# A query buffer of its own for the first cross unit of a layer, and its maxima dealt earlier

## The chip, the cores and the metric

The kernel runs on one core of one Trainium2 chip. The metric is the device time of one execution in microseconds (us), of which the median of three runs counts. The engines are named as the profile names them: PE is the matrix engine (PEld its weight loads), DVE the vector engine, ACT the scalar engine, POOL GpSimd, and SP the engine that only issues DMAs.

## The reference

Two layers of a transformer block run over four batches of 512 tokens with 320 features. Each layer has self attention, cross attention to a context of 1601 rows with 192 features, and a gated feed-forward part; each part has a layer norm before it and a residual add behind it. There are 20 heads of 16 features.

```python
h1 = _ln(x, n1_g, n1_b)
x = _attn(h1, h1, q1, k1, v1, o1_w, o1_b, heads) + x
h2 = _ln(x, n2_g, n2_b)
x = _attn(h2, context, q2, k2, v2, o2_w, o2_b, heads) + x
h3 = _ln(x, n3_g, n3_b)
a, g = jnp.split(h3 @ ff_w1 + ff_b1, 2, axis=-1)
ff = a * jax.nn.gelu(g, approximate=False) @ ff_w2 + ff_b2
return ff + x
```

`_attn` is softmax attention: `a = softmax(q k^T / 4)`, `out = a v`, and then `out @ wo + bo`. Queries times keys are kept nearly exact: a value is split into a high and a low part, and both are multiplied in the fast format fp32r.

## The kernel before

**Units.** The work of a layer is cut into 20 self units, 20 cross units and 4 feed-forward units. An attention unit is one batch and one group of four heads (five groups to a batch). A self unit has 4 chunks of 128 keys, a cross unit 13 (1601 keys). Below, self unit 0 to 19 and cross unit 0 to 19 are counted within a layer.

**What a unit needs.** Before a unit runs, three things are made for it: its queries (`queries`, L726 to L740) and keys (`keys`, L758, or `keys_of_context`, L801), each as matmuls, a copy to a staging tile, a split into high and low part on POOL (L627, L628) and DMAs on SP's queue into a query buffer and a key buffer; and the maximum of each query's scores, which softmax subtracts. For the maxima the scores are multiplied once with queries as rows (matmuls into tile `sps`, L957) and reduced by DVE (L978; L1000 for the last keys). `max_end` (L1029 to L1037) sends the maxima through a transpose and eight small DMAs into a row tile `m`.

**A unit's own run (`main`).** In each chunk the scores are multiplied again with keys as rows (tile `st`, L1144, two matmuls for each head), a third matmul subtracts the maxima (L1147), ACT takes the exponential into a place of a ring of buffers (L1157), and a chunk later the products with the values follow (tile `av`, L1171). The first chunk's product is copied into the unit's output tile `o` (L1182, on ACT); those of later chunks are copied to a place (L1187) and added by POOL (L1188). When the last chunk is added, `add_finish` transposes `o` on DVE, divides by the row sums, and four DMAs carry it from `o` to tile `aT` (L1072), from which the output projection reads (L1081). The tile `o` comes from a pool of three buffers.

**Maxima beside scores.** A chunk has two half rounds: scores of heads 0 and 1, then of heads 2 and 3. `giver` deals one group of maxima matmuls (four matmuls, two heads, one block of 512 keys) to each half round. They use the other half of the array's rows, so they run beside the scores. A self unit has 8 half rounds, and the next self unit has 8 groups of maxima, so the slots are just full. A cross unit has 26 groups. What does not fit is dealt as an extra round: two groups, eight matmuls, with no scores beside them, and three reductions on DVE (one of two heads, two of one head). The banks that they fill come from the pools `ps_m` (two double banks) and `ps_st` (four banks, which the scores and most other work also use).

**The first cross unit.** Cross unit 0 of each layer (`u.early`) needs 26 groups while only self units run before it. Its keys are due at the start of the unit four before it, with 16 rounds between the two pieces; its two query pieces are due at the start of the unit two before it (L847), since its query buffer is one of four that units take in turn, and is free only when the unit four before it in the order of attention has its scores (`unread`). In `giver`, maxima of this unit are dealt only when queries and keys have been made and moved for three rounds (`at_hand`).

**The planner.** Everything beside a unit's own run stands in queues (`add(chain, cost, f, due, ...)`). After each chunk `steps` takes pieces of work by due time as long as its credit lasts; `pace` sets the credit from the total of what is due. Each engine's order is thus fixed when the program is built.

Of the kernel before, what the change touches and what calls it, by code (L numbers as in the profile page):

```python
# [64 lines left out]
def kernel(ctx: ExitStack, tc: tile.TileContext, x, context, ws, out):  # L65
# [57 lines left out]
    def load_x(b):  # L123
# [33 lines left out]

    own = const.tile([P, 7, N], F32, name="pr")
    mine = [own[:, i, :] for i in range(7)]
    places = {  # L160
        "self": mine + [w1_flat[:, (2 * KB + 2) * D : (2 * KB + 2) * D + N], w1r[:, 4 * CTX : 4 * CTX + N]],
        "cross": mine + [wself[:, i * N : (i + 1) * N] for i in range(5)],
    }
    at_place = {"kind": "self", "i": -1}

    def place():
# [130 lines left out]
    for i, u in enumerate(attn):  # L297
# [10 lines left out]
        else:  # L308
            part = u.m % 4 if u.m < B * G - 1 else 0
            u.kT, u.k0 = (kbuf[0], part * N) if part < 3 else (kbuf[2], 0)  # L310
            u.other = attn[i - 3] if u.m == B * G - 1 else attn[i - 4] if u.m > 3 or u.m == 3 and u.l else None
        u.qbuf = qbuf[i % 4]
        u.mrow = mrows[i % 2]
# [359 lines left out]
    def add_proj(u):  # L673
# [5 lines left out]
        keys_due, apart = (  # L679
            (units[u.i - 4].start, 8) if u.early else (lead(u) - 5, 3) if u.m == 1 else (due - 10, 4)  # L680
        ) if u.cross else (due, 0)
# [153 lines left out]
        def unread():  # L835

            return u.n < 4 or attn[u.n - 4].scored == attn[u.n - 4].nch

# [4 lines left out]
        def add_queries():  # L843
            if u.g == 0 and u.cross:
                add(chain, 0.0, hold, due - 4, yes, lambda: "h" in u.own)
            for part in range(parts):
                add(chain, (0.05 + 0.427 / parts,) * 3, lambda part=part: queries(part), units[u.i - 2].start if u.early else due - 2, unread)  # L847

# [280 lines left out]
    def main(u, give, nxt):  # L1129
# [34 lines left out]
        def values(c):  # L1164
# [15 lines left out]
            if c == 0:  # L1180
                u.o = three.tile([P, N], F32, tag="o", name="o")
                (nc.vector.tensor_copy if last else nc.scalar.copy)(u.o, ps)  # L1182
            elif last:
                nc.vector.tensor_tensor(u.o, ps, u.o, ALU.add)
            else:
                vo = place()
                nc.scalar.copy(vo, ps)  # L1187
                nc.gpsimd.tensor_tensor(u.o, u.o, vo, ALU.add)  # L1188
# [58 lines left out]
    def ff_main(u, give, nxt):  # L1247
# [16 lines left out]
        hc = one.tile([P, 5, N], F32, tag="ctxT", name="hid")  # L1264
        hid = [hc[:, i, :] for i in range(5)]

        def full(c, pss, ahead):
# [24 lines left out]
        def gate(c, pss):  # L1292
            gl = mine[5 + c % 2]
            nc.scalar.activation(gl, pss[1], AF.Gelu, bias=b1[:, NHC + c : NHC + c + 1])  # L1294
# [231 lines left out]
```

## Time and profile before

| what | value |
|---|---|
| time, median of 3 runs | 3206.76 us (3204.16 to 6031.88) |
| span of the profiled execution | 3212.3 us |
| PE busy | 3036.1 us, 95% |
| DVE busy | 2093.8 us, 65% |
| ACT busy | 1963.7 us, 61% |
| POOL busy | 1267.8 us, 39% |

The profile gives the profiled execution's span, from its first to its last instruction, as its own time; nothing else of that execution is told. A unit's borders can be found in the trace by its score matmuls (L1144): a self unit has 32 of them, a cross unit 104. So a table of windows with such borders tells what each engine did while one unit ran. A row of it has the window and its length, then for PE, PEld, DVE, ACT and POOL the busy time and the number of instructions, then the clock that PE was granted (1.00 is full speed), the share of the DMA engines and the GB/s that they moved. Where the window table is asked for one line of the kernel alone, the busy times are those of that line.

### The profile page before, as it was taken

Reading aid. Unit: us, or ns where it says so; the run is one execution under the profiler, and the core shown is the slowest. Engines: PE = TensorE matmul, PEld = TensorE weight load, DVE = VectorE, ACT = ScalarE, POOL = GpSimd, SP = SyncE. Lnnn points to the kernel's source line nnn. Section 1 sums busy time; section 2 is a strip of 40 time slices with the busy share of each in tenths; the row PEclk is TensorE's granted clock in tenths of the full one; section 3 lists DMA queues with packets and bytes.
Section 4 is the critical chain, followed back from the end, with each engine's and each line's share of the span. In section 5 each row is a group of like instructions: output and inputs, shape, how many; then the busy total and the mean of one; then the engine's idle time right before and its main releaser. Section 6 shows DMA issues by size and latency. Waiting matters only on the chain.

```text
span 3212.3 us, 92658 instructions
## 1 busy us (share of the span) xinstructions
PE 3036.1 (95%) x37842; PEld 1644.5 (51%) x37842; DVE 2093.8 (65%) x2869; ACT 1963.7 (61%) x4029; POOL 1267.8 (39%) x1449
## 2 busy tenths in 40 slices
PE   8899899999999999999998998999999999999999
PEld 4455555555454555455454554555555555544555
DVE  6777778778678767522256777787777777784221
ACT  3666557777777778711136665587777778785110
POOL 3445334544544544211124453345454454442000
PEclk8999989999999999999999999999999999999999
DMA  4433212211211211200113322121111211212000
GB/s 96 94 71 77 54 37 49 59 37 40 56 38 38 57 35 27 85 1 5 27 30 78 73 60 52 39 53 40 32 46 40 40 44 34 40 23 66 9 11 15
DMA packets 256579, 145.32 MB, mean 45 GB/s; under 512 B 150037, under 2 KB 246681, under 8 KB 256153
## 3 DMA queue, kind: packets, MB, share of 16 engines
q1 hardware_dynamic: 254888, 138.33, 19.5%
q8 instruction: 298, 4.88, 0.7%
q10 hardware_dynamic: 1264, 1.06, 0.2%
q14 instruction: 129, 1.05, 0.1%
HBM read 33.04 MB, written 7.93 MB: 13 GB/s over the span
## 4 chain that ended last, share of the span: by engine, by line
PE 77%; DVE 6%; ACT 6%; SPq 4%; DMA 3%; issue 2%; POOL 1%; ACTq 0%; POOLq 0%; DVEq 0%
PE av L1171 19%; PE st L1144 16%; PE fps L1271 9%; PE st L1147 6%; PE yps L1327 5%; PE sps L957 4%; ACT pr L1157 3%; PE ops L1081 3%; PE qps L726 3%; PE kps L801 3%; PE vps L900 3%; DVE pm L978 2%; SPq L1037 2%; PE fps L1284 2%; DVE nmax L978 2%
## 5 line engine op out<-in xcount | busy, mean ns | idle before, releaser
L978 DVE TENSOR_REDUCE pm<-sps 128x2 f32<-128x1024 f32 (+1 forms) x980 | 1132.3, 1195 | 166.5 <-PE sps L957 155.6
L1157 ACT ACTIVATE pr<-st 128x512 f32<-128x512 f32 (+1 forms) x1710 | 906.7, 602 | 259.7 <-PE st L1147 250.6
L1144 PE MATMUL st<-q,kT 32*128 32x512 f32 (+1 forms) x5440 | 1001.0, 443 | 44.5 <-ACT w L810 26.8
L957 PE MATMUL sps<-kT,q 32*128 32x512 f32 (+1 forms) x6400 | 989.2, 410 | 31.2 <-DVE pm L978 11.3
L1188 POOL TENSOR_TENSOR o<-o,pr 128x512 f32<-128x512 f32 x359 | 461.2, 1285 | 750.4 <-ACT pr L1187 728.1
L1144 PEld LDWEIGHTS st<-q,kT 32*128 32x128 f32 (+1 forms) x5440 | 504.6, 184 | 471.3 <-ACT pr L1157 149.7
L1171 PE MATMUL av<-pr,vals 128*32 128x512 f32 (+1 forms) x3420 | 657.2, 629 | 40.5 <-ACT pr L1157 21.0
L1147 PE MATMUL st<-m,units 2*128 2x512 f32 (+1 forms) x2720 | 614.2, 402 | 24.4 <-DMA m<-turned 23.3
L1157 ACT ACTIVATE wself<-st 128x512 f32<-128x512 f32 (+1 forms) x867 | 462.9, 603 | 103.2 <-PE st L1147 101.6
L957 PEld LDWEIGHTS sps<-kT,q 32*128 32x128 f32 x6400 | 483.4, 190 | 68.7 <-DVE pm L978 27.8
L978 DVE TENSOR_REDUCE nmax<-sps 128x2 f32<-128x1024 f32 (+1 forms) x340 | 378.4, 1153 | 157.2 <-PE sps L957 117.2
L1171 PE MATMUL av<-wself,vals 128*32 128x512 f32 (+1 forms) x1734 | 376.3, 621 | 14.2 <-ACT pr L1157 14.0
L1188 POOL TENSOR_TENSOR o<-o,wself 128x512 f32<-128x512 f32 x191 | 245.2, 1284 | 342.1 <-ACT wself L1187 339.9
L1147 PEld LDWEIGHTS st<-m,units 2*128 2x128 f32 (+1 forms) x2720 | 313.4, 185 | 70.8 <-issue 30.9
L1271 PE MATMUL fps<-hT,w 128*128 128x512 f32 x640 | 285.3, 598 | 1.4 <-DVE hid L1297 0.9
L1294 ACT ACTIVATE pr<-fps,b 128x512 f32<-128x512 f32 x80 | 50.7, 684 | 385.4 <-PE fps L1284 274.6
L1187 ACT COPY pr<-av 128x512 f32<-128x512 f32 x359 | 217.1, 605 | 25.8 <-PE av L1171 24.2
L1171 PEld LDWEIGHTS av<-pr,vals 128*32 128x32 f32 (+1 forms) x3420 | 92.2, 109 | 215.3 <-ACT pr L1157 92.8
L1271 PEld LDWEIGHTS fps<-hT,w 128*128 128x128 f32 x640 | 118.5, 190 | 151.6 <-issue 145.6
L627 POOL TENSOR_SCALAR stage<-stage 128x256 fp32r<-128x256 f32 (+1 forms) x155 | 106.8, 689 | 193.9 <-ACT stage L734 97.9
L801 PEld LDWEIGHTS kps<-ctxT,w 32*128 32x128 f32 (+1 forms) x4992 | 115.4, 164 | 53.8 <-ACT pr L1157 28.7
L430 POOL TENSOR_SCALAR root<-root 128x4 f32<-128x4 f32 x23 | 5.2, 226 | 328.0 <-DVE root L424 327.7
(100 smaller groups left out, 3269.0 us busy)
## 6 DMA issues: line engine op xcount, KB each, us to landing
kT<-w SPq DMA_DIRECT2D x240, 104.0 KB
q<-stage SPq DMA_DIRECT2D x320, 64.0 KB
q<-stage SPq DMA_DIRECT2D x154, 128.0 KB
aT<-o SPq DMA_DIRECT2D x320, 32.0 KB
m<-turned SPq DMA_DIRECT2D x636, 2.0 KB
kT<-stage SPq DMA_DIRECT2D x156, 64.0 KB
kT<-w SPq DMA_DIRECT2D x80, 72.0 KB
w<-in_L_xattn_ff_w_dram SPq DMA_DIRECT2D x20, 256.0 KB
```

The source lines that it names most:

```text
L627: eng.tensor_scalar(high.bitcast(F32R), x, 1.0, None, ALU.mult)
L801: nc.tensor.matmul(ps[to : to + n, :PIECE], lhsT=wk_q[rows, k, u.g * GD : u.g * GD + n], rhs=first.kvT[rows, k, at : at + PIECE], start=(k ...
L957: nc.tensor.matmul(out, lhsT=u.q[rows, e, queries].bitcast(F32R), rhs=u.kT[rows, keys].bitcast(F32R), start=(e == 0), stop=(e == 1),)
L978: nc.vector.tensor_reduce(to[:, j : j + n], part, AX.X, ALU.max, negate=(ns == 1))
L1144: nc.tensor.matmul(st[:r, :], lhsT=keys, rhs=u.q[rows, e, :].bitcast(F32R), start=(e == 0), stop=False)
L1147: nc.tensor.matmul(st[:r, :], lhsT=units_of[two_rows, :r].bitcast(F32R), rhs=u.mrow[two_rows, :].bitcast(F32R), start=False, stop=True,)
L1157: nc.scalar.activation(p[:r], st[:r], AF.Exp)
L1171: nc.tensor.matmul(ps[j * SLOT : (j + 1) * SLOT, :], lhsT=columns_of[:r, head : head + SLOT], rhs=pr.pop((c, j))[:r, :], start=True, stop= ...
L1187: nc.scalar.copy(vo, ps)
L1188: nc.gpsimd.tensor_tensor(u.o, u.o, vo, ALU.add)
L1271: nc.tensor.matmul(ps, lhsT=w1[:, k, i * FF + c * P : i * FF + (c + 1) * P], rhs=u.hT[:, k, :], start=ahead and k == 0, stop=not ahead and ...
L1327: nc.tensor.matmul(ps[:, :D], lhsT=hid[c][:, t * P : (t + 1) * P], rhs=w2[:, c, :], start=(c == 0), stop=(c == NHC - 1),)
```

## The change

The kernel after has one more query buffer, `early_q`, for cross unit 0 of each layer. With it the wait on the unit four before goes (`unread`), its two query pieces are due at the start of the unit six before it and four rounds later, and its two pieces of keys at the start of the unit five before it and eight rounds ahead of that. The buffers are paid for with two others: the ring of places loses one of seven (`pr`), for which self units get a place in `w2`'s tile and cross units get none; and the output tiles `o` come from a pool of two buffers instead of three. The feed-forward part's second gate buffer, which was the seventh place, is now taken from the same pool of two.

```diff
-    own = const.tile([P, 7, N], F32, name="pr")
-    mine = [own[:, i, :] for i in range(7)]
+    own = const.tile([P, 6, N], F32, name="pr")
+    mine = [own[:, i, :] for i in range(6)]
     places = {
-        "self": mine + [w1_flat[:, (2 * KB + 2) * D : (2 * KB + 2) * D + N], w1r[:, 4 * CTX : 4 * CTX + N]],
+        "self": mine + [
+            w1_flat[:, (2 * KB + 2) * D : (2 * KB + 2) * D + N],
+            w1r[:, 4 * CTX : 4 * CTX + N],
+            w2_flat[:, 3 * D + 4 * kw : 3 * D + 4 * kw + N],
+        ],
         "cross": mine + [wself[:, i * N : (i + 1) * N] for i in range(5)],
     }
+    early_q = const.tile([P, 2, N], F32, name="early_q")
...
-        u.qbuf = qbuf[i % 4]
+        u.qbuf = early_q if u.early else qbuf[i % 4]
...
-            (units[u.i - 4].start, 8) if u.early else (lead(u) - 5, 3) if u.m == 1 else (due - 10, 4)
+            (units[u.i - 5].start, 4) if u.early else (lead(u) - 5, 3) if u.m == 1 else (due - 10, 4)
...
-            return u.n < 4 or attn[u.n - 4].scored == attn[u.n - 4].nch
+            return u.n < 4 or u.early or attn[u.n - 4].scored == attn[u.n - 4].nch
...
-                add(chain, (0.05 + 0.427 / parts,) * 3, lambda part=part: queries(part), units[u.i - 2].start if u.early else due - 2, unread)
+                add(chain, (0.05 + 0.427 / parts,) * 3, lambda part=part: queries(part), units[u.i - 6].start + 4 * part if u.early else due - 2, unread)
...
-                u.o = three.tile([P, N], F32, tag="o", name="o")
+                u.o = two.tile([P, N], F32, tag="o", name="o")
...
+        gls = [mine[5], two.tile([P, N], F32, tag="o", name="gl")]
...
-            gl = mine[5 + c % 2]
+            gl = gls[c % 2]
```

## The prediction

> **What bounds the kernel now.** I read the head of the page first, then the table of windows, with borders at the first score matmul of a unit, to find where the time of this change lies.
>
> ```profile
> span 3212.3 us, 92658 instructions
> PE 3036.1 (95%) x37842; PEld 1644.5 (51%) x37842; DVE 2093.8 (65%) x2869; ACT 1963.7 (61%) x4029; POOL 1267.8 (39%) x1449
> L1157 ACT ACTIVATE pr<-st 128x512 f32<-128x512 f32 (+1 forms) x1710 | 906.7, 602 | 259.7 <-PE st L1147 250.6
> L1188 POOL TENSOR_TENSOR o<-o,pr 128x512 f32<-128x512 f32 x359 | 461.2, 1285 | 750.4 <-ACT pr L1187 728.1
> L1294 ACT ACTIVATE pr<-fps,b 128x512 f32<-128x512 f32 x80 | 50.7, 684 | 385.4 <-PE fps L1284 274.6
> ```
>
> PE is busy 95% of the span, so over the whole kernel nothing but PE's gaps, and its time at a lowered clock, can be won. The next fence has layer 0's self units 4, 8, 12, and 14 to 19, then cross unit 0, and of layer 1 self unit 0 and self units 18 and 19. Columns: window, length, busy time and count of PE, PEld, DVE, ACT, POOL; then the granted clock, the DMA share and GB/s.
>
> ```profile
> 117.50:138.20 20.70, 18.46 (x205) 8.72 (x200) 17.40 (x25) 11.59 (x24) 6.98 (x7) 0.84 0.30 69
> 197.00:211.10 14.10, 13.23 (x188) 6.84 (x184) 12.26 (x21) 10.20 (x22) 6.36 (x7) 1.00 0.39 87
> 265.80:286.60 20.80, 19.97 (x396) 12.62 (x392) 15.45 (x29) 14.02 (x30) 13.34 (x18) 1.00 0.30 80
> 303.50:318.90 15.40, 14.71 (x212) 7.70 (x208) 12.80 (x18) 11.42 (x25) 7.72 (x8) 1.00 0.43 87
> 318.90:334.00 15.10, 13.18 (x164) 6.16 (x160) 11.25 (x16) 11.05 (x23) 6.96 (x7) 1.00 0.31 63
> 334.00:353.90 19.90, 17.89 (x308) 10.74 (x304) 13.59 (x20) 12.07 (x25) 6.44 (x6) 1.00 0.27 57
> 353.90:368.70 14.80, 13.80 (x228) 8.31 (x224) 10.03 (x15) 10.92 (x23) 6.30 (x9) 1.00 0.19 39
> 368.70:401.10 32.40, 26.70 (x476) 15.54 (x476) 27.34 (x37) 12.27 (x27) 11.66 (x12) 0.84 0.26 52
> 401.10:431.20 30.10, 27.34 (x372) 16.15 (x366) 20.52 (x33) 12.84 (x29) 4.26 (x4) 0.83 0.08 16
> 431.20:483.30 52.10, 48.22 (x750) 28.23 (x742) 38.28 (x47) 34.94 (x73) 24.80 (x23) 0.93 0.24 48
> 1647.10:1671.70 24.60, 22.07 (x233) 10.44 (x232) 20.86 (x27) 11.21 (x22) 4.47 (x6) 0.86 0.22 41
> 1977.30:2009.60 32.30, 27.17 (x474) 15.12 (x474) 27.29 (x37) 12.23 (x27) 11.04 (x11) 0.84 0.27 53
> 2009.60:2039.70 30.10, 27.45 (x373) 17.05 (x366) 20.54 (x33) 12.84 (x29) 4.87 (x6) 0.83 0.08 16
> ```
>
> Units 18 and 19 take 62.5 us in layer 0 and 62.4 in layer 1, where a plain self unit (unit 8) takes 14.1. DVE is busy 27.3 of unit 18's 32.4 us, and the clock is granted at 0.84 and 0.83. The same table for the maxima matmuls alone says why (units 17, 18, 19, columns PE and PEld):
>
> ```profile
> 353.90:368.70 14.80, 4.09 (x24) 1.98 (x24) 1.00 0.19 39
> 368.70:401.10 32.40, 11.22 (x80) 5.18 (x82) 0.84 0.26 52
> 401.10:431.20 30.10, 8.55 (x80) 4.47 (x80) 0.83 0.08 16
> ```
>
> A self unit has slots beside its scores for 32 maxima matmuls; units 18 and 19 have 80 each, so 48 each, six extra rounds of eight, stand alone. These are cross unit 0's. PE's waits in these two units (total, times, longest) and DVE's reductions there name the limit:
>
> ```profile
> PEld sps L957 <- DVE pm L978: 4.2, 5, 1.4
> PEld st L1144 <- DVE pm L978: 4.1, 5, 1.6
> L978 DVE TENSOR_REDUCE pm<-sps x36: 677/932/1227, 371.8 to 428.6; 128x2 f32<-128x1024 f32 x18, 128x1 f32<-128x512 f32 x18
> 377.12 0.86 PE L957 MATMUL sps<-kT,q 32*128 32x512 f32 x8 [0.63 <-DVE nmax L978]
> 316.20:318.90 2.70, 2.45 (x32) 1.15 (x28) 2.58 (x3) 1.94 (x5) 1.29 (x1) 1.00 0.12 22
> ```
>
> Scores (`st`) and maxima (`sps`) wait until DVE has emptied a bank. One extra round is 0.86 us of PE (fourth line, eight matmuls), but one reduction of two heads and two of one head on DVE, by the ends of the third line's range 1.23 + 2 x 0.68 = 2.6 us. The last line is a chunk with nothing beside its scores and eight maxima: 2.7 us, DVE busy 2.58.
>
> **The change part by part.** What the changed kernel's order of instructions shows (an order, no times): in self units 14 to 19 the maxima go from 32, 32, 32, 24, 80, 80 to 40, 40, 48, 48, 48, 48, in cross unit 0 from 136 to 144, in both layers alike. So 12 extra rounds in units 18 and 19 become 10 spread over units 14 to 19 (1, 1, 2, 2, 2, 2), unit 17's eight missing ones fill slots, and cross unit 0 gets a fifth round. Nothing is removed in sum; the question is the price of a round where it now stands.
>
> *Price where it stood.* The order gives each unit's other matmuls (all but scores, maxima, values). Unit 8 has 36 in 14.1 us, unit 12 has 144 in 20.8, both with 32 maxima: 6.7 / 108 = 0.062 us for one. Unit 18 has 156: without extra rounds 14.1 + 120 x 0.062 = 21.5, so its six cost 10.9, 1.8 each. Unit 19 has 102: 18.2, so 11.9 for six, 2.0 each. Together 22.8 us a layer. Unit 4 is unit 8 with two rounds more (36 others): 6.6, 3.3 each, at clock 0.84. Layer 1's unit 0 has 48 others and four rounds: (24.6 - 14.8) / 4 = 2.4, at 0.86.
>
> *Price where it goes.* Four of the ten stand in chunks with 24 to 48 other matmuls (one in unit 15, two in 16, one in 18). Such a chunk has 2.7 + 24 x 0.062 + 0.86 = 5.0 us of PE at least, and DVE has 2.58 + 2.6 = 5.2: DVE just fits, and I take PE's 0.86. Unit 19's two stand with 24 value matmuls, but 3.5 rounds in one chunk, so as before: 2.0. Four stand in chunks with 0 to 12 others (14, 17 twice, 18); there DVE sets the pace, and I take 2.6, DVE's own price, between 0.86 and unit 4's 3.3. Sum 4 x 0.86 + 2 x 2.0 + 4 x 2.6 = 17.8, so **-5.0 us a layer**; ends for all ten: 8.6 and 33. What is late next in units 18 and 19 is PE with 156 and 102 others, less what moved ahead.
>
> *Cross unit 0's fifth round*: 0.86 to 3.3; unit 18's price is nearest, **+1.8**. *Unit 17's slots*: nothing for PE, beside scores; DVE gets two reductions, 2.5 us, in a unit with 10.03 of 14.8 busy. If that cover failed it would be those 2.5.
>
> *Moved queries and keys.* The second piece of keys goes from unit 13 to 12, the queries from 17 to 13, the value matmuls of 16 to 18 a little: 0.062 each, which one unit loses and another gains, so zero. Their 16 DMAs are as many as before. In unit 14, SP's queue then holds eight query DMAs where six others stood, ahead of the eight that carry the maxima of unit 15; at some 0.65 us each (2.88 for four below) these come 1.3 us later. They hide behind the extra round of unit 14's chunk 2 (2.6); without it, 1.3.
>
> *Ring of places.* Cross units have 11 instead of 12, self units nine as before. The exponentials' idle time is ended by scores for 250.6 of 259.7 us (page rows above), none by POOL's add, the slow reader of a place. So nothing; if it did bind, one add, 1.3 us, per chunk.
>
> *Gate buffer of the feed-forward part.* Gelu waits for matmuls, 274.6 of 385.4 us (page row), and still alternates between two buffers: nothing.
>
> *Two output tiles instead of three.* This adds a wait: a unit's first copy into `o` (L1182, ACT) must wait for the four DMAs that empty the tile of the unit two before. They are issued in the same unit's first chunk. Behind the copy on ACT stand the exponentials, and PE's scores wait for their banks. Rows of SP and ACT in layer 0's unit 14 and layer 1's unit 4:
>
> ```profile
> 308.20 2.49 SPq L1072 DMA_DIRECT2D aT<-o  x4
> 311.83 0.62 ACT L1182 COPY o<-av 128x512 f32<-128x512 f32 x1
> 312.18 2.88 SPq L739 DMA_DIRECT2D q<-stage  x4
> 1733.20 4.18 SPq L1072 DMA_DIRECT2D aT<-o  x4
> 1734.18 0.62 ACT L1182 COPY o<-av 128x512 f32<-128x512 f32 x1
> 1740.28 4.63 SPq L1037 DMA_DIRECT2D m<-turned  x8
> 1747.28 2.07 ACT L1157 ACTIVATE pr<-st 128x512 f32<-128x512 f32 x4 [5.47 <-PE st L1147]
> PE st L1147 <- DMA m<-turned: 4.1, 1, 4.1
> ```
>
> The last issue for `m` ends at 1744.91, and the exponentials that need it start at 1747.28, so a DMA lands at most 2.4 us after its issue. Unit 14's copy starts 1.1 us after the last issue, so its wait is 0 to 1.3 us; neither end has a nearer row, and I take the middle, **+0.7** a layer. Layer 1's unit 4 would wait at least 3.2 us (1737.38 less 1734.18), but PE stands 4.1 us for the maxima's DMAs of the same queue a chunk or two later; the queue does not move, so the later wait shrinks by as much: 0, at most 5.
>
> By the Trainium skill, "DMA: Bandwidth & Descriptors", section "Anatomy of one DMA — SWDGE path", a DMA issued by GpSimd carries about 2 us of fixed cost, most of it the receipt of the last byte. The rows above, of SP's DMAs, agree so far as they bound a landing by 2.4 us. An estimate by that page puts unit 14's wait at 0.9 us, and the sum below 0.2 a layer higher.
>
> **Sum**: -5.0 + 1.8 + 0.7 = -2.5 a layer, -5.0 in two. From the profiled 3212.3 that is 3207.3; this execution is 5.5 us, 0.2%, above the median of 3206.8, from which it is **3202**.
>
> **The rivals.**
>
> *B, all is smoothed.* DVE has room everywhere, each round costs PE's 0.86: 8.6 - 22.8 + 0.86 = -13.3 a layer (the wait absorbed), 3180. For it: in units 14 to 17 DVE is busy 47.7 of 65.2 us. Against it: no unit with extra rounds in the trace has a price below 1.8.
>
> *C, each round trips the clock (slower).* Every unit with extra rounds in the fence, 4, 18, 19 and layer 1's 0, ran at 0.83 to 0.86, each self unit there without them at 1.00. If a round alone in a chunk makes PE wait long enough, six units a layer drop instead of two, and each round costs unit 4's 3.3: 33 + 3.3 - 22.8 + 0.7 = +14.2 a layer, 3235. It decides when the rounds' mean price passes 2.0, where eleven of them and the wait cost the 22.8 saved. Against it: unit 4 had both rounds in one chunk; the changed order has one to a chunk except in unit 19.
>
> The Trainium skill, "TensorE: Matmul & The Clock Gate", section "A second HAM failure mode: psum-queue depth-cycling", states that PE's short idles between groups of matmuls while banks cycle make the clock fall to half and rise again; taken alone, it speaks for this rival. The trace agrees as far as units with extra rounds go, 0.83 to 0.86.
>
> *D, the two output tiles bind everywhere.* If landing comes after the copy in all 36 self units from unit 2 on by unit 14's upper end, 1.3, and ACT passes it on, that is +47, and 3 in layer 1's unit 4; with -3.2 a layer from the rest 3250. Against it: ACT is idle 3.9 of unit 8's 14.1 us.
>
> *E, the maxima are not dealt earlier.* The order excludes it but for a wait on the moved DMAs: 3207.
>
> **How the numbers follow.** Forecast A (3190 to 3214) 0.53, B 0.18, C 0.21, D 0.05, E 0.03. The range 3181 to 3231 takes in A, E, and most of B and C, whose prices run from the forecast's to their ends; it leaves out some 0.07 of each and D. About 2%, 64 us, is what a measurement of this kernel can tell from no change; none of the cases reaches it: faster 0.02, same 0.95, slower 0.03.
>
> **What would show it.** In the changed kernel's windows, units 18 and 19 together near 47 us a layer (62.5 less 22.8, plus four rounds' 0.86 + 2.6 + 2 x 2.0), at a clock above 0.9; units 14 to 17 near 75 (65.2 plus six rounds' 3 x 0.86 + 3 x 2.6). If the clock of units 14 to 17 falls below 0.9, C is at work; if they stay below 70, B. L1182's idle time ended by DMAs into `aT` shows the two tiles' price: 2 us in all if right, over 20 if D. The prediction is wrong if something outside self units 12 to 19 and cross unit 0 moves by more than a few us.

## The result

The changed kernel takes **3220.3 us** (median of 20 runs, 3209.2 to 3231.2) against 3208.5 for the kernel before (20 runs beside it): a ratio of **1.0035 [1.0023, 1.0046]**. (One of the 20 runs of the kernel before took 6031.88 us; the ratio leaves it out.) It is slower by 12 us, far less than 2%, but clear of 1; I had forecast it 5 us faster. The time lies inside my range of 3181 to 3231, but the direction was wrong.

### The profile page after: what moved, and what is told of

Same layout as the page of the kernel before. It is cut to its first block, busy times and chain, and to the rows that moved or that the text cites. A ratio compares the mean times of both kernels' runs of the same rounds, so it can differ in the third digit from the quotient of the medians.

```text
span 3219.7 us, 92922 instructions
## 1 busy us (share of the span) xinstructions
PE 3030.0 (94%) x37842; PEld 1644.1 (51%) x37842; DVE 2097.1 (65%) x2867; ACT 1963.8 (61%) x4029; POOL 1269.3 (39%) x1449
## 4 chain that ended last, share of the span: by engine, by line
PE 76%; DVE 7%; ACT 5%; SPq 4%; DMA 3%; issue 2%; POOL 2%; ACTq 0%; DVEq 0%; POOLq 0%
PE av L1176 19%; PE st L1149 16%; PE fps L1277 9%; PE st L1152 6%; PE yps L1333 5%; PE sps L962 4%; PE kps L806 3%; PE ops L1086 3%; PE qps L731 3%; PE vps L905 3%; ACT pr L1162 3%; DVE pm L983 3%; PE fps L1290 2%; SPq L1042 2%; DVE nmax L983 2%
## 5 line engine op out<-in xcount | busy, mean ns | idle before, releaser
L983 DVE TENSOR_REDUCE pm<-sps 128x2 f32<-128x1024 f32 x975 | 1131.3, 1199 | 159.0 <-PE sps L962 147.1
L1149 PE MATMUL st<-q,kT 32*128 32x512 f32 (+1 forms) x5232 | 965.8, 443 | 55.9 <-ACT w L815 22.2
L962 PE MATMUL sps<-kT,q 32*128 32x512 f32 (+1 forms) x6144 | 960.0, 409 | 31.1 <-DVE pm L983 10.0
L1162 ACT ACTIVATE pr<-st 128x512 f32<-128x512 f32 (+1 forms) x1560 | 830.0, 602 | 244.8 <-PE st L1152 230.5
L1193 POOL TENSOR_TENSOR o<-o,pr 128x512 f32<-128x512 f32 x330 | 424.6, 1287 | 693.5 <-ACT pr L1192 660.1
L1162 ACT ACTIVATE wself<-st 128x512 f32<-128x512 f32 (+1 forms) x946 | 505.5, 603 | 104.4 <-PE st L1152 98.8
L1176 PE MATMUL av<-wself,vals 128*32 128x512 f32 (+1 forms) x1892 | 409.7, 616 | 19.3 <-ACT pr L1162 18.9
L1193 POOL TENSOR_TENSOR o<-o,wself 128x512 f32<-128x512 f32 x208 | 267.4, 1286 | 364.3 <-ACT wself L1192 362.8
L1300 ACT ACTIVATE pr<-fps,b 128x512 f32<-128x512 f32 x40 | 27.5, 688 | 385.4 <-PE fps L1290 274.6
L1192 ACT COPY pr<-av 128x512 f32<-128x512 f32 x330 | 199.9, 606 | 20.3 <-PE av L1176 19.4
L806 PE MATMUL kps<-ctxT,w 32*128 32x104 f32 (+1 forms) x4992 | 132.3, 278 | 2.7 <-DVE nmax L983 1.3
```

What stands on the lines that cost most here:

```text
L806: nc.tensor.matmul(ps[to : to + n, :PIECE], lhsT=wk_q[rows, k, u.g * GD : u.g * GD + n], rhs=first.kvT[rows, k, at : at + PIECE], start=(k ...
L962: nc.tensor.matmul(out, lhsT=u.q[rows, e, queries].bitcast(F32R), rhs=u.kT[rows, keys].bitcast(F32R), start=(e == 0), stop=(e == 1),)
L983: nc.vector.tensor_reduce(to[:, j : j + n], part, AX.X, ALU.max, negate=(ns == 1))
L1149: nc.tensor.matmul(st[:r, :], lhsT=keys, rhs=u.q[rows, e, :].bitcast(F32R), start=(e == 0), stop=False)
L1162: nc.scalar.activation(p[:r], st[:r], AF.Exp)
L1176: nc.tensor.matmul(ps[j * SLOT : (j + 1) * SLOT, :], lhsT=columns_of[:r, head : head + SLOT], rhs=pr.pop((c, j))[:r, :], start=True, stop= ...
```

## The profile after

The head of the page of the changed kernel:

```profile
span 3219.7 us, 92922 instructions
...
PE 3030.0 (94%) x37842; PEld 1644.1 (51%) x37842; DVE 2097.1 (65%) x2867; ACT 1963.8 (61%) x4029; POOL 1269.3 (39%) x1449
```

PE is busy 6.1 us less than before, in a span 7.4 us longer: PE stands idle more. The table of windows, with the borders and columns of the prediction: layer 0's self units 12 and 14 to 19 and cross unit 0, layer 1's self units 14, 15, 18 and 19.

```profile
263.00:284.90 21.90, 20.50 (x468) 13.23 (x464) 16.31 (x30) 14.23 (x31) 15.37 (x20) 1.00 0.30 80
302.40:330.80 28.40, 20.93 (x224) 9.94 (x220) 14.28 (x19) 12.10 (x25) 8.59 (x11) 0.82 0.29 58
330.80:349.60 18.80, 16.01 (x220) 7.85 (x216) 15.10 (x19) 11.73 (x24) 7.16 (x7) 1.00 0.37 76
349.60:373.40 23.80, 22.08 (x328) 11.99 (x324) 18.55 (x26) 11.60 (x23) 7.66 (x8) 0.93 0.21 43
373.40:391.80 18.40, 15.25 (x181) 7.83 (x177) 16.57 (x23) 9.91 (x19) 3.17 (x3) 0.91 0.11 23
391.80:410.40 18.60, 16.30 (x372) 9.44 (x368) 16.38 (x23) 11.67 (x26) 10.40 (x11) 1.00 0.15 32
410.40:430.50 20.10, 19.23 (x375) 13.48 (x372) 12.01 (x22) 12.56 (x29) 5.54 (x5) 1.00 0.30 58
430.50:483.00 52.50, 48.40 (x760) 28.81 (x756) 40.64 (x50) 35.35 (x74) 24.80 (x23) 0.97 0.24 48
1912.70:1938.50 25.80, 18.43 (x220) 8.92 (x216) 13.54 (x18) 12.02 (x25) 8.57 (x11) 0.87 0.27 55
1938.50:1959.60 21.10, 17.45 (x224) 8.58 (x220) 15.77 (x19) 11.79 (x24) 7.01 (x8) 0.92 0.32 66
1998.70:2018.00 19.30, 16.33 (x372) 9.40 (x368) 17.08 (x24) 11.67 (x26) 10.39 (x11) 1.00 0.15 32
2018.00:2039.60 21.60, 20.73 (x369) 14.22 (x368) 11.97 (x22) 12.57 (x29) 5.47 (x5) 0.92 0.28 53
```

Unit 12, which took over a piece of keys, has 1.1 us more. Units 18 and 19 fell to 38.7 and 40.9 us a layer, well below the 47 of the forecast. Units 14 to 17 rose from 65.2 to 89.4 us in layer 0, where the forecast was 75. Of these 24 us, 13 are in unit 14 alone: 15.4 before, 28.4 now, with the clock at 0.82; in layer 1 units 14 and 15 rose alike, from 15.4 and 17.5 to 25.8 and 21.1. Here is what ACT and PE wait for in this unit (us in total, times, longest):

```profile
ACT stage L739 <- DMA q<-stage: 4.3, 1, 4.3
ACT stage L771 <- DMA early_q<-stage: 3.0, 1, 3.0
...
ACT stage L739 <- DMA kT<-stage: 2.0, 1, 2.0
```

```profile
PE st L1149 <- ACT stage L739: 4.6, 2, 3.1
PE st L1149 <- ACT stage L771: 1.7, 1, 1.7
```

In the kernel before, ACT waits for no DMA in unit 14. Lines 739 and 771 are ACT's copies of fresh queries and keys from their bank into the tile `stage`, of which there are two; four DMAs then carry each piece on to its place. A copy must wait until the DMAs of the piece two before have emptied its tile. The timelines of SP and ACT show why that takes so long (start, length, operation; in brackets the idle time ahead and what ended it; rows left out are marked).

```profile
287.73 5.42 SPq L827 DMA_DIRECT2D kT<-w  x7
293.21 0.62 SPq L823 DMA_DIRECT2D kT<-w  x1
294.84 4.61 SPq L1042 DMA_DIRECT2D m<-turned  x8
...
300.94 3.11 SPq L744 DMA_DIRECT2D q<-stage  x4
304.16 2.68 SPq L776 DMA_DIRECT2D kT<-stage  x4
306.93 2.47 SPq L1077 DMA_DIRECT2D aT<-o  x4
309.50 5.30 SPq L744 DMA_DIRECT2D early_q<-stage  x8
321.78 4.62 SPq L1042 DMA_DIRECT2D m<-turned  x8
```

```profile
306.11 0.28 ACT L739 ACTIVATE stage<-qps 128x128 f32<-128x128 f32 x1 [4.26 <-DMA q<-stage]
308.41 0.28 ACT L739 ACTIVATE stage<-qps 128x128 f32<-128x128 f32 x1 [2.02 <-DMA kT<-stage]
317.41 0.37 ACT L771 COPY stage<-kps 128x256 f32<-128x256 f32 x1 [3.02 <-DMA early_q<-stage]
```

In these rows SP issues one DMA after the other, each in 0.6 to 0.8 us. POOL had split the two ordinary pieces by 293.15, but the DMAs that empty their tiles (300.94, 304.16) stand behind ten that carry the context keys (two of them in the rows left out), and behind the eight for the maxima. The two early query pieces come to ACT meanwhile. The first waits until 306.11, the second until 308.41, and the ordinary keys, at 317.41, for the early DMAs. Behind each copy in ACT's order stand the exponentials, and PE's scores wait for the banks that those empty. PE stands idle 7.5 us of this unit, where it was 0.7 in the kernel before; 6.3 of that are the waits above. It is also busy 6.2 us longer: 0.9 is the extra round, most of the rest the matmuls at the lower clock. That makes up the 13.0.

Behind the eight early DMAs SP then stands until 321.78 for maxima that DVE has not made yet, with the next piece's DMAs queued behind (SP's waits, the same columns):

```profile
SPq L1042 <- DVE turned L1036: 6.9, 1, 6.9
```

Outside units 12 to 19 and cross unit 0 little changed: self units 0 to 11 have 2 us more in both layers together, cross units 1 to 19 (3.2 us less in layer 0, 2.9 more in layer 1) and the feed-forward parts the same within a microsecond in sum.

## The experiments

Every kernel was timed beside the kernel before, and the ratios are to that. "Local" is the time of self units 12 to 19 and cross unit 0, both layers together, from one profiled execution: 435.0 us before, 440.9 in the changed kernel. Two such executions of one kernel can differ by some 5 us (430.4 and 425.7 for the place of their own below), so a local difference of that size says nothing.

### The buffers alone

The kernel before with the ring of places, the gate buffer and two output tiles of the change; queries and keys as before. The lines shown are against the changed kernel; the wait on the unit four before (`unread`) is back as well.

```diff
-        u.qbuf = early_q if u.early else qbuf[i % 4]
+        u.qbuf = qbuf[i % 4]
-            (units[u.i - 5].start, 4) if u.early else ...
+            (units[u.i - 4].start, 8) if u.early else ...
-   ..., lambda part=part: queries(part), units[u.i - 6].start + 4 * part if u.early else due - 2, unread)
+   ..., lambda part=part: queries(part), units[u.i - 2].start if u.early else due - 2, unread)
```

> The kernel before with the payments alone: six places in the ring instead of seven (self units get one in w2's tile), output tiles and the second gate buffer from a pool of two. Queries, keys and maxima of cross unit 0 stay as they were; the order of PE is the same. Theory S (in the changed kernel the early queries' staging stalls ACT in self unit 14, 10.4 and 7.8 us over what the extra round explains) expects no more than 3 us over the kernel before, 3208 to 3211. Theory D (two output tiles bind) expects at least 8 us of the 11.8 that the change lost, 3216 or more, with ACT's copies into o waiting for DMAs into aT.

3212.4 us, ratio 1.0012 [0.9996, 1.0028]: no measurable cost. The wait for an output tile exists where the prediction put it: ACT's copy into `o` waits 0.9 us in layer 0's unit 14 and 6.4 in layer 1's unit 4. First the windows of layer 1's self units 4 and 5 in the kernel before, then in this one:

```profile
1727.20:1741.40 14.20, 13.54 (x188) 6.92 (x184) 11.77 (x19) 11.18 (x24) 7.04 (x7) 1.00 0.39 53
1741.40:1762.80 21.40, 16.94 (x190) 7.93 (x186) 14.63 (x25) 11.46 (x24) 9.66 (x21) 0.84 0.24 48
```

```profile
1724.10:1746.10 22.00, 16.22 (x188) 8.16 (x184) 13.55 (x21) 11.23 (x24) 6.98 (x7) 0.84 0.34 55
1746.10:1760.70 14.60, 13.96 (x190) 7.06 (x186) 13.50 (x22) 11.38 (x24) 9.90 (x21) 1.00 0.28 57
```

Unit 4 takes 7.8 us longer and unit 5 6.8 less: the stall, and the low clock that goes with it, only come a unit earlier. In the kernel before, unit 5 has the clock at 0.84 without any extra round; its one long wait is PE's 4.1 us for the maxima's DMAs, which the prediction shows.

### A place of their own for the early pieces

The two early query pieces are staged in a stretch of the weight tile `w2`, which at other times holds a piece of context keys, instead of in the pair `stage`; nothing else moves.

```diff
-            high, low, both = stages()
+            if u.early:
+                empty("stage", 1)
+                room = w2_flat[:, 3 * D + 2 * kw : 3 * D + 2 * kw + N].rearrange("p (e n) -> p e n", e=2)
+                both = room[:, :, part * w : (part + 1) * w]
+                high, low = both[:, 0], both[:, 1]
+            else:
+                high, low, both = stages()
```

> The changed kernel, with cross unit 0's two query pieces staged in a free part of w2's tile instead of the pool of two staging tiles; every engine's order but for the tile is as in the changed kernel. Theory S expects ACT's waits in self unit 14 to go, that unit to fall from 28.4 and 25.8 us to 18 to 20, and the whole by 14 to 18 us, to 3203 to 3206, somewhat under the kernel before. Theory C (each extra round alone trips the clock) expects unit 14 to keep its half clock and the whole within 4 us of the changed kernel's 3220.

> e2_own_stage once more, without any edit; with e12_own_group_again it tells whether the ratios 0.9979 and 1.0002 of two kernels that spend the same time in self units 12 to 19 and cross unit 0 (321.8 + 108.5 and 324.4 + 106.3 us by their profiles) differ by the kernel or by the call. If by the kernel: 0.998 and 1.000 again. If by the call: both within 0.998 to 1.000 and less than 0.001 apart.

3201.6 us, 0.9979 [0.9966, 0.9991]; measured again on another chip, 3205.4 us, 0.9986 [0.9973, 0.9999]. This is faster than both kernels, by far less than 2% but clear of 1 both times, and some 16 to 18 us below the changed one by its ratio. The windows of unit 14 in both layers, and its waits of ACT for a DMA (the first line; PE's is the second):

```profile
304.30:323.40 19.10, 16.18 (x220) 8.24 (x217) 13.97 (x19) 11.65 (x24) 8.44 (x11) 1.00 0.37 79
...
1904.10:1924.40 20.30, 17.68 (x223) 8.63 (x219) 13.71 (x18) 11.76 (x24) 8.43 (x11) 0.92 0.39 83
```

```profile
ACT stage L777 <- DMA kT<-stage: 2.8, 1, 2.8
```

```profile
PE st L1155 <- ACT stage L777: 1.4, 1, 1.4
```

Unit 14 is shorter by 9.3 and 5.5 us, and its clock is back at 1.00 and 0.92 with the same extra round in it. So the clock fell for the stall, not for the round (the next runs show the opposite case, a stall without a round). Local is 430.4 us, 10.5 less than in the changed kernel; in the profiled executions cross units 1 to 19, which the edit doesn't touch, have another 14.6 less (below).

### Maxima dealt late, with and without the place

The maxima of cross unit 0 are withheld until self unit 18, so that nothing is spread; once with the shared pair, once with the place of their own.

```diff
-  hand = [v for v in ahead if left(v) and all(v.pairs) and at_hand(v)]
+  hand = [v for v in ahead if left(v) and all(v.pairs) and at_hand(v) and not (v.early and u.kind == "self" and u.m < 18)]
-                if mine and not alone and at_hand(v):
+                if mine and not alone and at_hand(v) and not (v.early and u.kind == "self" and u.m < 18):
```

> The changed kernel, with cross unit 0's maxima withheld until self unit 18, so that units 18 and 19 have the 80 maxima matmuls each of the kernel before; queries and keys stay early. It takes the spreading alone away. Theory S expects unit 14 to stay slow by about 10 us, units 18 and 19 back at some 62 us, units 14 to 17 shorter by the rounds' price, so 15 to 25 us more than the changed kernel's 3220 less some 15 for the rounds: 3225 to 3232. Theory C, by which the spreading is the loss, expects the kernel before's time, 3208, or less.

> The changed kernel with the maxima of cross unit 0 withheld until self unit 18 (as e4_late_dealing, 3239.2 us) and the early queries staged in a place of their own (as e2_own_stage, 3201.6). With the changed kernel (3220.3) and those two this completes a table of two by two. If the two effects add up: 3239.2 - 18.7 = 3220.5. If the staging tiles were all that the early queries cost: the time of the kernel before with a fifth round in cross unit 0, 3210 to 3214. If the tiles matter only where the maxima are dealt early as well: 3235 to 3239. Unit 14 in each layer: 16 to 20 us in the first two cases, 24 in the third; units 18 and 19 together 60 us in all of them.

3239.2 us, 1.0099 [1.008, 1.0119], and 3223.0 us, 1.0040 [1.0024, 1.0057]. With the two kernels above they make a table of two by two (local in us from the windows; ratio):

| | shared pair | own place |
|---|---|---|
| maxima from unit 14 on | 440.9; 1.0035 | 430.4; 0.9979 and 0.9986 |
| maxima from unit 18 on | 460.6; 1.0099 | 447.1; 1.0040 |

The windows of units 12 to 19, layer 0 and then 1, in the kernel before, the changed kernel, and the last two (shared, own):

```profile
265.80:431.20 165.40, 149.71 (x2388) 86.23 (x2386) 123.28 (x183) 97.52 (x205) 69.09 (x82) 0.94 0.26 56
1871.60:2039.70 168.10, 152.52 (x2449) 87.75 (x2446) 122.07 (x181) 96.01 (x203) 65.80 (x78) 0.93 0.25 50
```

```profile
263.00:430.50 167.50, 147.01 (x2375) 83.49 (x2372) 122.67 (x177) 97.26 (x204) 69.56 (x82) 0.95 0.26 55
1872.80:2039.60 166.80, 144.10 (x2429) 83.23 (x2428) 121.31 (x175) 95.58 (x202) 65.89 (x78) 0.96 0.25 50
```

```profile
265.40:445.60 180.20, 157.69 (x2381) 89.49 (x2378) 124.71 (x182) 98.01 (x204) 69.38 (x82) 0.91 0.24 51
1888.50:2067.80 179.30, 156.66 (x2438) 89.08 (x2435) 122.56 (x179) 96.01 (x202) 65.92 (x78) 0.90 0.23 47
```

```profile
267.10:439.00 171.90, 154.09 (x2381) 87.08 (x2378) 124.98 (x182) 97.94 (x204) 69.25 (x82) 0.93 0.25 54
1880.60:2050.50 169.90, 151.09 (x2439) 87.80 (x2438) 122.74 (x179) 95.83 (x202) 65.88 (x78) 0.93 0.24 49
```

The two effects add up, within the scatter. The shared pair costs 10.5 and 13.5 us by the windows (16 to 19 by the ratios), whether the maxima are spread or not. The spreading wins 19.7 and 16.7 us (17 to 21 by the ratios), with cross unit 0's fifth round paid. What is left, 447.1 less 435.0, is 12 us (1.0040, 13 us): the early queries, the earlier keys and the buffers that pay for them cost this together, with a place of their own and nothing spread. The runs don't separate them; the buffers alone had 3.7 us in these windows and 1.0012. In unit 15 of that kernel PE waits 1.3 us for the maxima's DMAs in layer 0 and 3.9 us for those of keys in layer 1; both stand behind the eight early ones in SP's queue.

Unit 14 of the shared pair with nothing spread settles the clock. It has 32 maxima matmuls, so no extra round:

```profile
304.80:329.90 25.10, 18.46 (x213) 8.70 (x208) 12.21 (x16) 11.93 (x25) 8.64 (x12) 0.86 0.30 60
...
1928.10:1952.70 24.60, 18.55 (x212) 8.81 (x208) 11.52 (x15) 11.93 (x25) 8.54 (x12) 0.79 0.23 47
```

The stall without a round has the clock at 0.86 and 0.79; with the place of their own and no round it is 1.00 in both layers, in 17.4 and 16.6 us.

### The two pieces apart

The changed kernel, its second early piece held back from the first by nine more chunks.

```diff
-   ..., units[u.i - 6].start + 4 * part if u.early else due - 2, unread)
+   ..., units[u.i - 6].start + 4 * part if u.early else due - 2, unread, (lambda part=part: clock["round"] >= units[u.i - 6].start + 4 + 9 * part) if u.early else yes)
```

> The changed kernel, with the two query pieces held back to rounds 4 and 13 after the start of self unit 14, so that they come one in unit 14 and one in unit 15, from the pool of two staging tiles. Theory S expects each piece to wait for one pair of DMAs instead of two pieces waiting in a row: the stall of unit 14 falls to a half or less, some 8 to 12 us from the whole, 3208 to 3212, with small stalls in units 14 and 15. Theory C expects about 3220.

3217.2 us, 1.0029 [1.0016, 1.0042]: a miss. Unit 14 fell only to 24.4 and 21.4 us. In layer 0 the ordinary queries and keys wait there 2.0 and 4.8 us for their tiles, before the first early piece comes to ACT at 317.83: the keys need DMAs that stand behind those of an output tile, and all stand behind the context keys. So SP's order stalls the pair even where no early piece is in it. Unit 18 rose to 24.2 and 24.8 us, as the maxima wait for the later piece: units 18 and 19 have 56 maxima matmuls each instead of 48.

### The queue: late, early, elsewhere

Is it the number of tiles, or the time until SP empties them? First the early DMAs are issued by POOL, at the same places in the program's order, with the shared pair and with the place of their own. Then SP issues them at once, ahead of what else the next chunks bring, again with both. Last a third tile.

```diff
-                queue = (nc.sync, nc.scalar)[s] if start["on"] else nc.sync
+                queue = nc.gpsimd if u.early else (nc.sync, nc.scalar)[s] if start["on"] else nc.sync
```

> The changed kernel (ratio to before 1.0035), in which the eight DMAs that carry the early queries of a layer out of the shared staging tiles are issued by POOL, right behind POOL's own split of the piece, and not by SP; the order on PE, DVE and ACT is the same. Theory F (ACT's copies into the staging tiles wait because the DMAs that empty them stand in SP's one queue behind others): the tiles come free earlier, ACT's waits for staging DMAs in unit 14 fall from some 10 us to 4 or less, and most of the 18 us of e2_own_stage come back, ratio 0.998 to 1.000. Rival T (two tiles are too few however soon their DMAs are issued): waits and time as in the changed kernel, 1.003 to 1.004. Rival P (issuing costs POOL more than SP, and POOL's splits and adds come late): 1.005 or more, with POOL's idle time gone in unit 14.

> e2_own_stage (ratio 0.9979) with the early queries' DMAs issued by POOL as in e9_pool_queue. Theory F: the eight DMAs leave SP's queue, where unit 14's ordinary staging copies still wait for some 6 us; unit 14 falls from 19 to 20 us to some 17, ratio 0.996 to 0.997. Rival T: nothing left to win, 0.998. Rival P: 1.000 or more.

With the shared pair, 3239.2 us, 1.0094 [1.0077, 1.0112]. Nothing of what I had hoped for came back. The time is that of rival P, but not by its mark, as POOL is busy only 13.4 of unit 14's 36.3 us. POOL's splits of the two pieces end at 308.58 and 310.89, but the DMAs don't come right behind them, where I had expected them: the first four are queued behind an add that itself waits 3.2 us for ACT, and the others behind the split of a later piece. POOL has issued them by 317.87 and 323.85, where SP had issued all eight by 314.80. ACT's waits in unit 14, and the units' windows in both layers:

```profile
ACT stage L771 <- DMA early_q<-stage: 5.6, 1, 5.6
ACT stage L739 <- DMA early_q<-stage: 5.4, 1, 5.4
ACT stage L739 <- DMA q<-stage: 4.3, 1, 4.3
```

```profile
303.40:339.70 36.30, 22.46 (x224) 10.24 (x220) 14.28 (x19) 12.14 (x25) 13.37 (x19) 0.76 0.23 46
1930.20:1967.40 37.20, 22.71 (x220) 10.43 (x217) 13.79 (x18) 12.14 (x25) 13.21 (x19) 0.77 0.23 46
```

Tiles emptied later make unit 14 longer, by 7.9 and 11.4 us: the same mechanism with the other sign. With the place of their own the same DMAs on POOL harm nothing: 3206.9 us, 0.9996 [0.9985, 1.0007], units 12 to 19 at 157.4 and 158.6 us, the shortest local time but one. The total is no better than that of the place alone: its profiled execution has 10 us more in self units 0 to 11 and 19 more in cross units 1 to 19, whose order the edit leaves as it was. That comparison overstates the difference: the profiled execution took 3218.6 us, 12 above its kernel's median, and that of the place alone 3194.1, 7.5 below.

```diff
-        if start["on"]:
+        if start["on"] or any(u.early for u in us) and name in ("qwhen", "qpart"):
             empty(kind, 0)
```

> The changed kernel with the shared pair of staging tiles (ratio 1.0035), the early queries' DMAs still issued by SP, but each piece's four at once behind the copies, ahead of whatever else would enter SP's queue in the next chunks. Theory F (ACT's copies wait because the DMAs that empty the two tiles stand late in SP's one queue): the tiles come free earlier, unit 14 falls from 28.4 and 25.8 us to 18 to 22, ratio 0.998 to 1.001. Rival T (two tiles are too few however soon their DMAs are issued): unit 14 stays above 24, ratio 1.003 to 1.004. If SP, which now waits for POOL's split at the head of its queue, makes the maxima's DMAs late: waits for those in unit 15 of 2 us or more, ratio above 1.004.

> e2_own_stage (ratios 0.9979 and 0.9986) and e13_issue_at_once (0.9999) in one: a place of their own for the early queries, and their DMAs, with those of the ordinary piece before them, issued at once, so that the ordinary piece no longer stands behind the eight for the maxima. Theory F: e2_own_stage's unit 14 and e13_issue_at_once's unit 15 together, 18 + 17.6 us against 40 in e2_own_stage: some 4 us a layer, ratio 0.996 to 0.9975. If the two edits took away the same wait, nothing more: 0.998 to 0.999. If SP's wait for POOL's split makes the maxima's DMAs late: waits for those in unit 15, 0.999 or more.

With the shared pair, 3208.5 us, 0.9999 [0.9986, 1.0011]: the order of the queue alone brings back nearly all of the 12 us lost. But not where I had said. Unit 14 fell only to 25.1 and 25.6, which was rival T's mark: in layer 0 its first two waits, 4.6 and 2.0 us, are for pieces that were queued earlier and behind the context keys. The third wait is gone, SP no longer holds the next piece behind the maxima, and unit 15 falls to 17.6 in both layers. With the place of their own as well, 3200.2 us, 0.9977 [0.9962, 0.9991], no measurable gain over the place alone. Now the output tiles show, ACT and then PE in unit 14:

```profile
ACT o L1193 <- DMA aT<-o: 4.5, 1, 4.5
```

```profile
PE st L1155 <- ACT o L1193: 3.5, 1, 3.5
```

The four DMAs that empty an output tile moved from ahead of the eight for the early queries to behind them, from 308.79 with the place alone to 314.75, and the wait that I had priced at 0.7 became 3.5.

For the third tile the pair is joined, from self unit 13 on, by the same stretch of `w2`, all pieces in turn. The kernel leaves out keeping it apart from the context keys: a piece of them shares this stretch at times and is overwritten there, so part of the cross units' keys has other content. The number of matmuls is the same.

```diff
-    def stages(kind="stage"):
-        empty(kind, 1)
+    def stages(kind="stage", third=False):
+        if third:
+            turn["third"] += 1
+            empty(kind, 2)
+            if turn["third"] % 3 == 0:
+                t = w2_flat[:, 3 * D + 2 * kw : 3 * D + 2 * kw + N].rearrange("p (e n) -> p e n", e=2)
+                return [t[:, e] for e in range(2)] + [t]
+        else:
+            empty(kind, 1)
```

> The changed kernel with a third staging tile from self unit 13 on, taken in turn by all pieces, early queries and ordinary ones. Theory F and rival T both: ACT's waits for staging DMAs in units 14 and 15 fall to under 2 us, units 14 and 15 together from 47.3 and 46.8 us to 35 to 38 a layer, ratio 0.996 to 0.999 and no worse than e2_own_stage (0.9979, 0.9986 again). If what is left of the loss after e2_own_stage is not the staging: units 14 and 15 stay at 40, ratio 0.998 to 1.000.

3213.7 us, 1.0010 [0.9993, 1.0026]; units 14 and 15 took 43.1 and 44.2 us together, not 35 to 38, with waits of 4.0 us in layer 0 and 2.8 in layer 1 for `q<-stage` left. One tile more is not enough while SP empties them in its own order; and as the third place is not free of context keys, this run settles no more than that.

### Slots, and earlier keys

The early pieces' DMAs in a group of slots of their own (no flush of the ordinary pieces); the context keys three units earlier still; both; and the group issued at once.

```diff
-    groups = {"stage": deque(), "kstage": deque()}
+    groups = {"stage": deque(), "kstage": deque(), "early": deque()}
-                "qwhen" if part == parts - 1 else "qpart",
+                "qwhen" if part == parts - 1 else "qpart", "early" if u.early else "stage",
```

```diff
-            (units[u.i - 5].start, 4) if u.early else ...
+            (units[u.i - 8].start, 4) if u.early else ...
```

> The staging place of the early queries as in e2_own_stage (3201.6 us), and their DMAs in a group of slots of their own, so that no ordinary staging copy is held back behind them in the order. Theory S (the loss was ACT's copies waiting for the shared staging tiles): nothing more to win there, 3201 +-4 us, unit 14 of each layer at 19 to 20 us as in e2_own_stage. Theory Q (what is left of it, unit 14 at 19.1 and 20.3 us against 15.4 before, is SP's one queue, where the ordinary pieces' DMAs still stand behind eight early ones and eight of the maxima): the order of the queue hardly changes, so the same 3201. Rival R (the placing of the copies in ACT's order was a part of it): unit 14 falls to some 16 us in both layers, 3194.

> e5_own_group once more, without any edit: 1.000 if its difference from e2_own_stage lies in the kernel, 0.9985 to 0.9995 if it lay in the call.

> e2_own_stage, with the keys of the context for cross unit 0 made eight units ahead instead of five (unit 12's first chunk), and the queries with them one chunk later. Theory Q (the keys' and queries' DMAs standing side by side in SP's queue are what unit 14 still waits for): the keys' DMAs leave units 13 and 14, unit 14 falls by 3 us a layer, 3196. Theory S (only the shared staging tiles): 3201, unit 14 still at 19 to 20 us. If the keys now crowd unit 12 and 13 instead: 3203 to 3207, with the time found in those units.

> e5_own_group and e6_keys_earlier together. Theory Q: the sum of the two, 3194 to 3196. Theory S: 3201.

> e5_own_group (1.0002 and 1.0022) with the early DMAs issued at once; the ordinary pieces keep their turn. Theory F: unit 14 and 15 together some 2 to 4 us a layer below e5_own_group's 43.3 and 41.1, ratio 0.998 to 1.000. If nothing is left: 1.000 to 1.002.

The group: 3212.3 us, 1.0002 [0.9984, 1.0021], and again 3213.2, 1.0022 [1.0009, 1.0034]. The keys earlier: 3211.7, 0.9996 [0.9983, 1.0009]; unit 14 stayed at 20.3 and 21.4 us, units 12 and 16 of layer 0 rose to 23.3 and 27.3 and unit 13 of layer 1 to 24.0. Both: 3208.9, 0.9994 [0.9979, 1.0008]. The group at once: 3210.9, 0.9998 [0.9984, 1.0011], unit 14 at 29.7 us in layer 0 and 18.8 in layer 1. None gains on the place of their own alone. The expectations of the first and of both with earlier keys were missed: in unit 14 they are near the place of their own, in the total they are not.

### The cross units behind

The place of their own and the group of slots differ by 10.7 and 7.8 us in the medians of two pairs of measurements. In the first pair of profiles their local times are alike (430.4 and 430.7 us), and the difference stands in cross units 1 to 19, whose matmuls are the same. Their windows, layer 0 and layer 1, for the own place and then the group:

```profile
481.10:1343.90 862.80, 818.63 (x11694) 443.66 (x11690) 648.14 (x807) 668.45 (x1386) 410.68 (x418) 0.98 0.21 47
2078.60:2912.20 833.60, 802.70 (x11688) 437.65 (x11684) 633.59 (x765) 666.18 (x1383) 410.62 (x418) 0.99 0.20 44
```

```profile
484.00:1356.50 872.50, 827.00 (x11694) 448.23 (x11690) 648.36 (x807) 668.61 (x1386) 410.76 (x418) 0.96 0.21 47
2088.60:2929.70 841.10, 809.98 (x11689) 441.75 (x11685) 633.98 (x765) 666.17 (x1383) 410.42 (x418) 0.98 0.20 44
```

PE is busy 15.7 us more with the same matmuls, at a lower granted clock. In the second pair these units took 1700.5 and 1710.8 us, but 13 us more stood in self units 0 to 11 and 6 in the local part. And both profiled executions of the place alone lie below their kernel's median, by 7.5 and 14 us, so they are not typical of it. Whether this hangs on the moment at which the cross units are entered was tried by matmuls that nobody reads, four and twelve, ahead of cross unit 1 of layer 0 (each goes as two on PE):

```diff
+        if u.cross and u.l == 0 and u.m == 1:
+            warm(4)
         (ff_main if u.kind == "ff" else main)(u, giver(u), nxt)
```

> e2_own_stage with four more matmuls, whose result nobody reads, on PE ahead of cross unit 1 of layer 0: 2.4 us by 0.6 each. The cross units behind are the same. If their time doesn't hang on the moment at which they are entered: e2_own_stage (3201.6 and 3205.4) plus 2.4, ratio 0.9987 to 0.9994. Rival H (the granted clock in the cross units depends on the moment, which is how e2_own_stage and e5_own_group come to differ by 9 us behind equal stretches): cross units 1 to 19 with another half-clock time, and a ratio that moves by 0.001 to 0.004 to either side of that.

> As e15_four_idle with twelve matmuls, 7.2 us. If the moment doesn't matter: e2_own_stage plus 7.2, ratio 1.0002 to 1.0010. Rival H: 0.001 to 0.004 to either side.

The trace prices them at 3.7 and 10.6 us. Measured: 3212.8 us, 1.0004 [0.9991, 1.0017], and 3218.2 us, 1.0033 [1.0015, 1.0050]. From 0.9979 to 0.9986 the added work alone leads to 0.9991 to 0.9998, which the first interval holds, and to 1.0012 to 1.0019, of which the second holds the upper part. In the profiled executions layer 0's cross units 1 to 19 took 875.7 and 870.6 us against 862.8 and 865.2, at an unchanged order. That could point to the moment of entry, but these two lie 3 and 8 us above their kernels' medians where the other two lie below, and the medians don't decide it: this stays open, and with it up to 10 us of any single comparison here.

## Why the prediction was wrong

**The step that failed** is "Moved queries and keys", which the prediction closed with "so zero". It counted the queue's delay for the maxima alone ("these come 1.3 us later") and never asked who else waits for these DMAs: the next pieces, for their two staging tiles. In unit 14 four pieces take their turn in the pair instead of two, and the copies on ACT, which carry the stall on to the scores, wait 9.3 us. By the two-by-two table this costs 10 to 14 us in the units and 16 to 19 in the total, and with the pair still shared a better order in SP's queue alone brings back nearly all of the 12 us lost (0.9999). Another 12 us stay with the early queries and keys, and the buffers that pay for them, even with a place of their own and nothing spread; units 12 and 13 have 3.1 us more in both layers together, 14 and 15 have 12, units 16, 19 and cross unit 0 have 7, and units 17 and 18 have 10 less. How these 12 us divide between the three wasn't measured. A price of 0.062 us for each matmul moved contains no wait, and this was the prediction's mistake.

**Mis-sized: the rounds.** Spreading was put at -5.0 a layer and the fifth round at +1.8, -6.4 in all; the table gives -17 to -20. Units 18 and 19 fell by 23.8 and 21.5 us where I took 22.8 less 7.5 for four remaining rounds: the four cost little where they now stand, and the clock went back to between 0.92 and 1.00. Layer 0's unit 18 has its two in two chunks, 0.84 and 0.85 us of PE with 0.64 idle before each. What stands alone in its unit 19, where I priced two rounds at 2.0 each, are 32 short matmuls for the last 66 keys, 1.8 us in all.

**Right:** the ring of places and the gate buffer, so far as the buffers alone have no measurable cost, and in layer 1's unit 4 the wait for an output tile, absorbed a unit later. The 0.7 in layer 0's unit 14 was 0.9 us of ACT with the buffers alone; in the changed kernel this copy doesn't wait for its tile, since the stall makes it come later. All waits of this kind there come to 5.6 us on ACT, where 2 were named: 3.8 in layer 1's unit 4, 1.1 and 0.7 in layer 0's units 2 and 7.

**The rivals.** B, all smoothed, falls in units 14 to 17 (89.4 us), though its -26.7 in both layers lay nearer to what the spreading alone gave than my -6.4. C had the sign right, by another cause. By its own mark, a clock below 0.9, it is at work in unit 14; but the same round goes with a clock of 1.00 and 0.92 in the kernel with the own place, and the stall without a round with 0.86 and 0.79, so it is the stall that lowers the clock there. The Trainium skill, "TensorE: Matmul & The Clock Gate", section "A second HAM failure mode: psum-queue depth-cycling", which was weighed with C, states that frequent short idles of PE between groups of matmuls make the clock swing between half and full. Two extra rounds in a unit did not do that in unit 18, at 1.00 in both layers; units 16 and 17, with two as well, had 0.93 and 0.91 in layer 0. So unit 14's low clock is not of this kind, and for units 16 and 17 this stays open. D falls with the buffers alone, 1.0012. E falls with the late dealing, which costs 20 us more.

So the sum was two large terms, -17 to -20 and +22 to +31, of which I had seen a third of the first and nothing of the second.

## What to carry to other kernels

When work is moved earlier, list every buffer that it passes through, and for each the queue that empties it: a pair of staging tiles behind one DMA queue is a resource with a place in time, even where bytes and matmuls stay the same. Where one engine carries in its order the copies and also the critical exponentials, as ACT here, one late DMA stalls both. A place of its own for the moved piece was enough here to make the change pay.

## What the hardware showed that I had not expected

- A small DMA from tile to tile takes SP 0.6 to 0.8 us to issue, four in 2.5 to 3.1 us and eight in 5.3, one after the other; ACT's copy into the emptied tile starts 1.6 to 2.6 us after the last issue (306.84 to 308.41, and 314.80 to 317.41).
- Moving the issue to a less busy engine was no gain by itself: on POOL the same DMAs were queued behind an add and a split and the last of them issued 9 us later (1.0094 against 1.0035).
- With PE waiting for ACT's copies, the clock of unit 14 was 0.79 to 0.87 with an extra round or without; without these waits it was 0.92 to 1.00 with the round.
- The same matmuls in the same order took 1696 or 1714 us in cross units 1 to 19, at granted clocks of 0.98 to 0.99 or 0.96 to 0.98, in executions of kernels that differ only ahead of them. Whether the kernel or the single execution decides this isn't shown.
